# Wave angles as 32-bit integers: one wrapping GpSimd product per tile in place of a two-step turn on GpSimd and VectorE

## The chip, the cores and the metric

The kernel runs on one core of one Trainium2 chip. The metric is the device time of one execution in microseconds (us). A core has five engines that run their own instruction streams in order: PE (TensorE, matrix products), DVE (VectorE), ACT (ScalarE), POOL (GpSimd) and SP (SyncE, which here only issues DMAs). They wait for each other through semaphores.

## The reference, cut to what matters

Sixteen images of 3 x 512 x 512 are cut into 1024 patches each, embedded to 256 features, and go through one transformer layer: attention with 8 heads of 32, then a small mixture of networks. What is unusual is the key. Before attention every key element x (1024 tokens x 256 features per image) is replaced by a Fourier sum over 256 frequencies:

```python
h = patches(x) @ W.T + b
q, k, v = split(layernorm(h) @ w_qkv)
k = sum(a[f] * sin((f + 1) * k) + b[f] * cos((f + 1) * k) for f in range(256))
h = h + softmax(q @ k.T / sqrt(32)) @ v @ w_out + b_out      # 8 heads
h = h + shared_mlp(layernorm(h)) + top2_experts(layernorm(h))
```

The kernel writes a frequency as a slow part (16 steps) and a fast part (8 steps), so that 16 x 16 products of slow and fast waves give all 256 terms.

## The kernel before, in words

**Tiles of waves.** The key's angle, as a fraction of a turn, is stored in DRAM (`ud`) as `u` and as `uh = u + 0.5` (lines 256 to 271, here called the key chunks: four per image, each 128 x 512, a chain of eight DVE instructions and two stores from SP's queue). Four features are one *group*; an image has 32 groups. For each group SP loads three tiles `w` of 128 x 1024 (lines 507 to 525): the same eight rows, repeated over the partitions. Two are for slow waves (one DMA each), the third for fast waves (two DMAs of 64 partitions). There are 12 buffers `w`, which is four groups.

**Turning a tile.** Each partition has its own frequency `f`. A tile must become `f*u` less its whole part. That takes two steps: `begin_turns` (L544) computes `t = w*f + ROUND` on POOL (or on DVE for some tiles), which leaves the nearest whole number in the low bits of `t`; `end_turns` (L534) computes `w*f - whole` on DVE. `t` has two buffers, so POOL cannot be more than two tiles ahead of DVE. Then ACT takes the sine (L556), PE mixes the slow waves with the coefficients (`mix`, L562, into one of two PSUM buffers `big`), DVE multiplies by the fast wave (`times_fast`, L572, which also frees that PSUM buffer), and PE adds up (`add_up`, L588).

**Rounds.** The main loop (lines 714 to 782) is an order written out by hand; each engine executes its instructions in this program order. One round is four groups and one attention step (two heads, half of the queries). An image has eight rounds, numbered 0 to 7 below. A round has a *sine phase* (for each group: three sines, `mix`, `times_fast`, `add_up`, and the loads that refill the freed buffers) and an *exponential phase* (eight steps of `score` L610, `exponential` L620, `weigh` L628). The attention step of two rounds earlier is used, so that keys are always a little ahead. In the exponential phase the tiles of the next round are turned: ten by POOL and DVE there, two by DVE alone in the sine phases of groups 1 and 2.

**Beginning of a round.** After the first three sines ACT copies the finished attention sums out of PSUM (`leave`, L642), and POOL copies two stripes of 32 x 512 of it (L644). In every second round (0, 2, 4, 6) DVE then normalizes (`normalize`): a reciprocal (L653), four products of 32 x 512 (L656) and one more pass (L661). These stand ahead of the first `times_fast` of the round on DVE.

**Pieces.** Everything else (the embedding of the next image, its layernorms, the key chunks, the networks of the image before) is cut into pieces that are slipped between these steps: the networks and their gate in rounds 2 to 5, the next image's tokens and key chunks in rounds 5 to 7. A layernorm uses POOL for a power (L189) and for adding a row (L210), and DVE for four scalings `hn` (L193).

Of the kernel before, what the change touches and what calls it, by code (L numbers as in the profile page):

```python
# [11 lines left out]
FP = mybir.dt.float32  # L12
AF = mybir.ActivationFunctionType
ALU = mybir.AluOpType
# [4 lines left out]
P = 128  # L19
E = 256  # L20
NPAIR = 4
HD = 32
N = 1024
# [14 lines left out]
TURN = 6.283185  # L38

ROUND = 1.5 * 2.0**23  # L40
BAND0 = 88
XT = 256
XBUFS = 2
# [2 lines left out]
NW = 12  # L46
GS = 4
# [4 lines left out]
def plain_path(ctx: ExitStack, tc: tile.TileContext, a: dict, out: bass.AP, verdict: bass.AP):  # L52
# [8 lines left out]
    nc = tc.nc  # L61
# [8 lines left out]
    const = pool("const", 1)  # L70
# [3 lines left out]
    udp = pool("udp", 2, DRAM)  # L74
    kup = pool("kup", 1)
    wp = pool("wp", NW)
    tp = pool("tp", 2)
# [11 lines left out]
    def load(shape, src, name):  # L89
        t = const.tile(shape, FP, tag=name, name=name)  # L90
        nc.sync.dma_start(out=t, in_=src)
        return t
# [29 lines left out]
    sel = load([NE, 2, P], a["sel"], "sel")  # L122
    gw = load([P, 2, NE], halves(a["gW"]), "gw")
    gbr = row_everywhere(a["gb"], NE, "gbr")
    lane = load([P, 2], a["waves"], "lane")
    f_slow, f_fast = lane[:, 0:1], lane[:, 1:2]
    pack = load([P, PACK0 + HD], a["pack"], "pack")
    ident = const.tile([P, P], FP, tag="ident", name="ident")
    make_identity(nc, ident)
# [84 lines left out]
    def tokens(b, st):  # L214

        hs = st["h"] = []
        for half in range(2):
            h = hp.tile([P, 4, E], FP, tag="h", name="h")
            hs.append(h)
            for pr in range(2):  # L220
                ps = side_tile("tok").rearrange("p (t e) -> p t e", e=E)
                for t in range(2):
                    j, col = divmod((4 * half + 2 * pr + t) * P, XT)
                    for c in range(NKC):
                        nc.tensor.matmul(  # L225
                            out=ps[:, t, :],
                            lhsT=chunks[b, j][:, c, ds(col, P)],
                            rhs=wt[:, c, :],
                            start=(c == 0),
                            stop=(c == NKC - 1),  # L230
                        )
                    if col + P == XT:
                        del chunks[b, j]
                        load_x(b, j + XBUFS)
                    yield
                nc.vector.tensor_add(
                    h[:, ds(2 * pr, 2), :], ps, tokb.unsqueeze(1).to_broadcast([P, 2, E])
                )
            yield from transposed_layernorm(h, half)
            add_row(h, bout)  # L240


        ud = st["ud"] = udp.tile([E // 4, 2, 4, N], FP, tag="ud", name="ud")
        for rows in range(2):
            for blk in range(2):
                ps = side_tile("k")
                for c in range(2):
                    nc.tensor.matmul(
                        out=ps,
                        lhsT=wk[:, c, ts(rows, P)],  # L250
                        rhs=hnT[:, c, ts(blk, 512)],
                        start=(c == 0),
                        stop=(c == 1),
                    )
                yield
                n = kup.tile([P, 512], FP, tag="n", name="turns")
                nc.vector.tensor_scalar(n, ps, INV_2PI, ROUND, ALU.mult, ALU.add)
                nc.vector.tensor_scalar(n, n, ROUND, None, ALU.subtract)
                r = kup.tile([P, 512], FP, tag="r", name="r")
                nc.vector.scalar_tensor_tensor(r, n, -TWO_PI_A, ps, ALU.mult, ALU.add)  # L260
                nc.vector.scalar_tensor_tensor(r, n, -TWO_PI_B, r, ALU.mult, ALU.add)
                nc.vector.scalar_tensor_tensor(r, n, -TWO_PI_C, r, ALU.mult, ALU.add)
                u = kup.tile([P, 512], FP, tag="u", name="u")
                nc.vector.tensor_scalar(u, r, INV_2PI_REST, None, ALU.mult)
                nc.vector.scalar_tensor_tensor(u, r, INV_2PI, u, ALU.mult, ALU.add)
                uh = kup.tile([P, 512], FP, tag="n", name="uh")
                nc.vector.tensor_scalar(uh, u, 0.5, None, ALU.add)
                for i, x in enumerate((uh, u)):
                    nc.sync.dma_start(
                        out=ud[ts(rows, P // 4), i, :, ts(blk, 512)], in_=x  # L270
                    )
            st["rows"] = rows + 1
        yield
# [228 lines left out]
    total = B * NG  # L502
    w_tiles = {}
    w_turns = {}
    ptr = {"load": 0, "turn": 0, "used": 0}

    def load_waves():

        while ptr["load"] < min(3 * total, ptr["used"] + NW):
            i = ptr["load"]  # L510
            g, j = divmod(i, 3)
            b, g = divmod(g, NG)
            st = images.get(b)
            if st is None or st.get("rows", 0) <= g // (NG // 2):
                return
            w = wp.tile([P, N], FP, tag="w", name="w")
            for s in range(1 + j // 2):
                m = 16 // (1 + j // 2)
                src = st["ud"][2 * g + (s if j == 2 else j)].rearrange("f e n -> (f e) n")
                nc.sync.dma_start(  # L520
                    out=w[ds(8 * m * s, 8 * m), :],
                    in_=src.unsqueeze(0).to_broadcast([m, 8, N]),
                )
            w_tiles[i] = w
            ptr["load"] += 1

    late = []

    def end_turns():

        while late:
            w, t, f = late.pop(0)
            whole = t.bitcast(mybir.dt.int16)[:, ::2]
            nc.vector.scalar_tensor_tensor(w, w, f, whole, ALU.mult, ALU.subtract)  # L534

    def begin_turns(engine):
        i = ptr["turn"]
        if i >= 3 * total:
            return
        assert i in w_tiles, i  # L540
        w = w_tiles[i]
        f = f_fast if i % 3 == 2 else f_slow
        t = tp.tile([P, N], FP, tag="t", name="t")
        engine.tensor_scalar(t, w, f, ROUND, ALU.mult, ALU.add)  # L544
        late.append((w, t, f))
        ptr["turn"] += 1


    kan = {}
    red = {}  # L550

    def sines(g):
        assert ptr["turn"] >= 3 * g + 3 and not late
        for j in range(3):
            w = w_tiles[3 * g + j]
            nc.scalar.activation(w, w, AF.Sin, scale=TURN)  # L556

    def mix(g):
        ps = kan[g] = big.tile([P, N], FP, tag="big", name="kan")
# [76 lines left out]
    def leave(qb):  # L636

        av = acc[0]
        if qb == 0:
            acc["sums"] = ffp.tile([P, 512], FP, tag="sums", name="sums")  # L640
        acc["v", qb] = ff2.tile([P, 512], FP, tag="avs", name="avs")
        nc.scalar.copy(acc["v", qb], av)  # L642
        for s in range(2):
            nc.gpsimd.tensor_copy(  # L644
                acc["sums"][ds(64 * qb + HD * s, HD), :],
                acc["v", qb][ds(HD + HD * s, HD), :],
            )
# [27 lines left out]
        load_x(0, j)  # L675
    run(tokens(0, image(0)))
    load_waves()
    for i in range(10):
        begin_turns(nc.vector)
        end_turns()  # L680

    RI = NG // GS
    plan = {"gen": None, "left": 0, "slots": 0, "need": None}
# [30 lines left out]
    with tc.manual_schedule():  # L714
        for rd in range(rounds + 2):
# [20 lines left out]
            for n, g in enumerate(groups):  # L736
                sines(g)
                if n == 0 and att > 0:
                    leave(qq)
                mix(g)  # L740
                if n == 0 and att > 0 and qq == 1:
                    normalize(pp)
                if n > 0:
                    times_fast(groups[n - 1])
                    add_up(groups[n - 1])
                    load_waves()
                if n in (1, 2):
                    end_turns()
                    begin_turns(nc.vector)
                    end_turns()  # L750
                piece("sin")
            if not groups and att > 0:
                leave(qq)
# [6 lines left out]
            for n in range(NT):  # L760
                if 0 <= att < 2 * NPAIR * B:
                    score(p, qb, n)
                    exponential(n)
                if n == 0 and groups:
                    add_up(g)
                if n == 2 and groups and g % 8 == 7:
                    finish_keys(g // 8)
                if 0 <= att < 2 * NPAIR * B and n >= 2:
                    weigh(p, qb, n - 2)
                end_turns()  # L770
                for _ in range(2 if n in (3, 7) else 1):
                    if ptr["turn"] < 3 * min(total, GS * (rd + 2)):
                        end_turns()
                        begin_turns(nc.gpsimd)
                piece("exp")
            if 0 <= att < 2 * NPAIR * B:
                for n in (6, 7):
                    weigh(p, qb, n)
            end_turns()
        leave(1)  # L780
        normalize(NPAIR * B - 1)
        run(networks(B - 1, images[B - 1]))
# [667 lines left out]
def _waves():  # L1450

    lane = np.arange(128)
    return np.stack([16.0 * (lane // 8) + 8.5, lane % 64 // 8 + 0.5], 1).astype(np.float32)


def _pack():
# [60 lines left out]
```

## Time and profile before

| what | value |
|---|---|
| times of three runs | 6951.01, 6960.5, 6960.35 us; median 6960.35 us |
| the profiled execution | 6941.8 us, of which the span from first to last instruction is 6940.3 us |
| busy: PE, DVE, ACT, POOL | 87%, 62%, 48%, 33% of the span |
| granted TensorE clock, mean | 0.913 |
| DMA queue of SP | 54.7% of 16 engines' span, 842.66 MB |
| turning, POOL part (L544) | 1270 instructions, 1820.9 us |
| turning, DVE part (L534 and L544) | 1536 and 266 instructions, 2229.2 and 219.6 us |
| copies of the attention sums on POOL (L644) | 256 instructions, 185.5 us |

How to read it: a busy share says how long an engine had an instruction in work, not that it set the time; PE's ends are modelled. The mean duration of a group mixes instructions that ran freely with some that were held up by another engine. A wait is put down to the engine whose result came last.

### The profile page before, as it was taken

To read this page: it belongs to the slowest core of one execution; us is meant where nothing else is said; L and a number is where in the kernel's file an instruction comes from. 1 tells how busy PE (TensorE), PEld (TensorE's weight loads), DVE (VectorE), ACT (ScalarE), POOL (GpSimd) and SP (SyncE) were. 2 spreads that over 40 slices of the span, in tenths; PEclk is the share of its full clock that TensorE was granted. 3 is DMA by queue.
4 is the path that set the end of the run, shared out by engine and by line. 5 is a ranking of instruction groups with operands and counts; after the bars stand their busy time and mean duration, and the time that the engine had idled before them with its cause. 6 is when DMAs were issued, how large, how long until landed. Compare 5 with 4: busy or idle time off the path is not lost.

```text
span 6940.3 us, 62611 instructions
## 1 busy us (share of the span) xinstructions
PE 6014.1 (87%) x21377; PEld 2081.1 (30%) x21377; DVE 4301.0 (62%) x4785; ACT 3319.5 (48%) x3773; POOL 2274.3 (33%) x1728
## 2 busy tenths in 40 slices
PE   5788888888898989989889898898988889888898
PEld 2223323233232323323233232332323323233223
DVE  4675665756657566565765657666575665756652
ACT  2364454544545445454453544545454454544553
POOL 2343333323323333332333323334232332333330
PEclk7899999999999989999899998999989899998998
DMA  6575564655656565565655755556566564655650
GB/s 163 143 166 131 128 148 114 153 114 140 148 114 151 111 144 135 130 151 111 146 126 128 155 115 139 130 124 149 124 143 131 123 147 112 155 124 122 147 123 10
DMA packets 264922, 913.86 MB, mean 132 GB/s; under 512 B 31241, under 2 KB 35218, under 8 KB 264594
## 3 DMA queue, kind: packets, MB, share of 16 engines
q1 hardware_dynamic: 246674, 842.66, 54.7%
q0 software_dynamic: 17920, 67.12, 3.3%
q8 instruction: 171, 2.80, 0.2%
q14 instruction: 157, 1.29, 0.1%
HBM read 859.32 MB, written 50.33 MB: 131 GB/s over the span
## 4 chain that ended last, share of the span: by engine, by line
PE 52%; DVE 15%; DMA 12%; issue 7%; ACT 7%; POOL 6%; SPq 0%; POOLq 0%; ACTq 0%; DVEq 0%
DMA w<-ud 11%; PE sT L610 10%; PE kan L562 8%; PE av L628 7%; PE red L588 6%; PE tok L225 5%; PE e3p L486 4%; PE e1p L411 3%; DVE rc L653 3%; POOL t L544 3%; ACT w L556 3%; DVE aT L656 2%; PE s1p L411 2%; PE q L279 2%; DVE w L534 1%
## 5 line engine op out<-in xcount | busy, mean ns | idle before, releaser
L544 POOL TENSOR_SCALAR t<-w,lane 128x1024 f32<-128x1024 f32 x1270 | 1820.9, 1439 | 2718.5 <-DVE w L534 1866.5
L534 DVE SCALAR_TENSOR_TENSOR w<-w,lane,t 128x1024 f32<-128x1024 f32 x1536 | 2229.2, 1471 | 719.8 <-POOL t L544 710.7
L620 ACT ACTIVATE es<-sT 128x1024 f32<-128x1024 f32 x1024 | 1041.9, 1023 | 2025.4 <-PE sT L610 2023.5
L556 ACT ACTIVATE w<-w 128x1024 f32<-128x1024 f32 x1536 | 1512.3, 1048 | 499.7 <-DVE w L534 495.0
L562 PE MATMUL kan<-w,coef 128*64 128x512 f32 x4096 | 1205.0, 643 | 111.0 <-ACT w L556 110.9
L610 PE MATMUL sT<-q,k 32*128 32x512 f32 x4096 | 1214.7, 671 | 21.8 <-ACT es L620 21.8
L628 PE MATMUL av<-es,v 128*64 128x512 f32 x4096 | 1129.9, 647 | 0.0
L588 PE MATMUL red<-prod,pack 128*32 128x512 f32 x2048 | 610.1, 678 | 502.0 <-DVE prod L572 501.4
L572 DVE TENSOR_TENSOR prod<-kan,w 128x1024 f32<-128x1024 f32 x512 | 625.4, 1221 | 513.4 <-PE kan L562 510.6
L562 PEld LDWEIGHTS kan<-w,coef 128*64 128x64 f32 x4096 | 305.4, 144 | 924.8 <-issue 497.9
L610 PEld LDWEIGHTS sT<-q,k 32*128 32x128 f32 x4096 | 320.0, 191 | 702.7 <-issue 518.7
L628 PEld LDWEIGHTS av<-es,v 128*64 128x64 f32 x4096 | 229.4, 141 | 778.0 <-issue 762.6
L653 DVE RECIPROCAL rc<-sums 128x512 f32<-128x512 f32 x64 | 214.6, 3353 | 389.3 <-POOL sums L644 389.3
L644 POOL COPY sums<-avs 32x512 f32<-32x512 f32 x256 | 185.5, 725 | 731.6 <-ACT avs L642 724.0
L620 ACT ACT_TABLE_LOAD x126 | 161.7, 1283 | 518.0 <-PE sT L610 517.4
L225 PE MATMUL tok<-wt,x 128*128 128x256 f32 x1536 | 394.5, 410 | 13.0 <-DMA x<-in_xT 12.5
L588 PEld LDWEIGHTS red<-prod,pack 128*32 128x32 f32 x2048 | 77.3, 113 | 944.0 <-DVE prod L572 625.5
L225 PEld LDWEIGHTS tok<-wt,x 128*128 128x128 f32 x1536 | 304.3, 205 | 169.1 <-issue 85.1
L411 PE MATMUL e1p<-hnT,w1e 128*128 128x512 f32 x512 | 271.5, 656 | 14.0 <-ACT e L471 12.9
L544 DVE TENSOR_SCALAR t<-w,lane 128x1024 f32<-128x1024 f32 x266 | 219.6, 826 | 10.5 <-DMA w<-ud 10.4
L496 POOL DMA_DIRECT2D out<-h x32 | 26.5, 828 | 591.1 <-DVE h L495 564.2
L495 DVE TENSOR_TENSOR h<-e3p,h 128x512 f32<-128x512 f32 x64 | 44.3, 692 | 269.5 <-PE e3p L486 269.5
(98 smaller groups left out, 4327.7 us busy)
## 6 DMA issues: line engine op xcount, KB each, us to landing
w<-ud SPq DMA_DIRECT2D x1024, 512.0 KB
w<-ud SPq DMA_DIRECT2D x1024, 256.0 KB
x<-in_xT POOLq DMA_DIRECT2D x64, 768.0 KB, 8.3
ud<-u SPq DMA_DIRECT2D x64, 256.0 KB
ud<-uh SPq DMA_DIRECT2D x64, 256.0 KB
out<-h POOLq DMA_DIRECT2D x32, 512.0 KB, 7.5
wt<-in_tok_wT SPq DMA_DIRECT2D x1, 768.0 KB
w1e<-in_eW SPq DMA_DIRECT2D x1, 512.0 KB
```

The costliest lines, as they stand in the source:

```text
L225: nc.tensor.matmul(out=ps[:, t, :], lhsT=chunks[b, j][:, c, ds(col, P)], rhs=wt[:, c, :], start=(c == 0), stop=(c == NKC - 1),)
L411: nc.tensor.matmul(out=ps, lhsT=lhsT(c), rhs=hnT[:, c, cols], start=(c == 0), stop=(c == 1),)
L534: nc.vector.scalar_tensor_tensor(w, w, f, whole, ALU.mult, ALU.subtract)
L544: engine.tensor_scalar(t, w, f, ROUND, ALU.mult, ALU.add)
L556: nc.scalar.activation(w, w, AF.Sin, scale=TURN)
L562: nc.tensor.matmul(out=ps[ts(j, 64), ts(blk, 512)], lhsT=coef, rhs=w_tiles[3 * g + j][:, ts(blk, 512)], start=True, stop=True,)
L572: nc.vector.tensor_mul(prod, kan.pop(g), w_tiles[3 * g + 2])
L588: nc.tensor.matmul(out=rows_of_pair[p][ds(64 * blk + HD * (r // 4), HD), :], lhsT=pack[:, o : o + HD], rhs=prod[:, ts(blk, 512)], start=(r ...
L610: nc.tensor.matmul(out=ps[:, ts(s, 512)], lhsT=k[rows, ts(kc, P)], rhs=q[p % NPAIR // 2][rows, ts(qb, 512)], start=True, stop=True,)
L620: nc.scalar.activation(es, scores.pop(kc), AF.Exp, scale=SCALE)
L628: nc.tensor.matmul(out=acc[0][ts(s, 64), :], lhsT=v[:, kc, p % NPAIR, ds(HD * s, 64)], rhs=es[:, ts(s, 512)], start=(kc == 0), stop=(kc == ...
L653: nc.vector.reciprocal(rc, sums)
```

## The change

- The angle is kept as a 32-bit integer, a full turn being 2^32. In each key chunk the last DVE instruction makes `ui = u * 2^31` with an integer output (half a turn per unit), and `uh = ui + 2^30` is now an integer addition on POOL.
- A tile is turned by one instruction on POOL: the integer product `w * f`, where `f` is one odd integer per partition, broadcast along the tile. It is meant to wrap at 32 bits, which drops the whole turns. `begin_turns`, `end_turns`, the tiles `t` and all turning on DVE are gone.
- ACT reads the integer tile and scales by 2*pi/2^32.
- The order changes: all 12 tiles of the first round are turned ahead of the loop; then one tile is turned in each sine phase of groups 2 and 3, and ten in the exponential phase (steps 6 and 7 turn two). All of these are POOL's.
- The two copies of the attention sums in `leave` move from POOL to DVE.

```diff
-                uh = kup.tile([P, 512], FP, tag="n", name="uh")
-                nc.vector.tensor_scalar(uh, u, 0.5, None, ALU.add)
-                for i, x in enumerate((uh, u)):
+                ui = kup.tile([P, 512], INT, tag="r", name="ui")
+                nc.vector.tensor_scalar(ui, u, 2.0**31, None, ALU.mult)
+                uh = kup.tile([P, 512], INT, tag="n", name="uh")
+                nc.gpsimd.tensor_tensor(uh, ui, quarter.to_broadcast([P, 512]), ALU.add)
+                for i, x in enumerate((uh, ui)):
...
-    def end_turns():
-        while late:
-            w, t, f = late.pop(0)
-            whole = t.bitcast(mybir.dt.int16)[:, ::2]
-            nc.vector.scalar_tensor_tensor(w, w, f, whole, ALU.mult, ALU.subtract)
-    def begin_turns(engine):
...
-        t = tp.tile([P, N], FP, tag="t", name="t")
-        engine.tensor_scalar(t, w, f, ROUND, ALU.mult, ALU.add)
-        late.append((w, t, f))
+    def turn_waves(n):
+        for _ in range(n):
...
+            f = lane[:, i % 3 // 2 : i % 3 // 2 + 1]
+            nc.gpsimd.tensor_tensor(w, w, f.to_broadcast([P, N]), ALU.mult)
...
-            nc.scalar.activation(w, w, AF.Sin, scale=TURN)
+            x = w_tiles[3 * g + j] = w.bitcast(FP)
+            nc.scalar.activation(x, w, AF.Sin, scale=TURN * 2.0**-32)
...
-            nc.gpsimd.tensor_copy(
+            nc.vector.tensor_copy(
                 acc["sums"][ds(64 * qb + HD * s, HD), :],
...
-    for i in range(10):
-        begin_turns(nc.vector)
-        end_turns()
+    turn_waves(NW)
...
-                if n in (1, 2):
-                    end_turns()
-                    begin_turns(nc.vector)
-                    end_turns()
+                if n >= 2:
+                    turn_waves(1)
...
-                end_turns()
-                for _ in range(2 if n in (3, 7) else 1):
-                    if ptr["turn"] < 3 * min(total, GS * (rd + 2)):
-                        end_turns()
-                        begin_turns(nc.gpsimd)
+                if ptr["turn"] < 3 * min(total, GS * (rd + 2)):
+                    turn_waves(2 if n > 5 else 1)
```

## The prediction

> **What bounds the kernel now.** The busy shares come first (the page's first part), then PE's own waits, then the eight rounds of one image as windows, then the rows of the instructions that the change touches.
>
> ```profile
> PE 6014.1 (87%) x21377; PEld 2081.1 (30%) x21377; DVE 4301.0 (62%) x4785; ACT 3319.5 (48%) x3773; POOL 2274.3 (33%) x1728
> ```
> ```profile
> PE red L588 <- DVE prod L572: 501.4, 96, 15.3
> PE kan L562 <- ACT w L556: 110.9, 128, 10.4
> PE wT L429 <- DVE gwt L354: 104.4, 16, 6.6
> PE lnT L205 <- DVE hn L193: 83.0, 65, 7.3
> PE k L248 <- DVE r L260: 56.2, 15, 5.7
> ```
> PE is the bound: only 6940 - 6014 = 926 us are idle. Over half of that is one wait, `red` for `prod`, 96 times: six per image. The 111 us on ACT are 128 waits of 0.9 us, one per round, at the change from exponentials to sines; they stay.
>
> Windows of one image, rounds 0, 1, 4 and 7 (busy PE, PEld, DVE, ACT, POOL; then granted clock, DMA share, GB/s):
> ```profile
> 3010.50:3056.20 45.70, 36.16 (x124) 9.61 (x124) 32.59 (x27) 23.76 (x25) 19.83 (x14) 0.93 0.75 161
> 3056.20:3092.60 36.40, 35.48 (x144) 11.14 (x140) 19.32 (x16) 25.62 (x34) 12.35 (x11) 1.00 0.74 157
> ...
> 3204.90:3270.30 65.40, 58.94 (x193) 19.35 (x190) 33.91 (x30) 29.16 (x35) 16.05 (x13) 0.95 0.50 105
> ...
> 3394.90:3437.50 42.60, 32.91 (x120) 7.93 (x116) 30.57 (x31) 24.36 (x27) 15.62 (x11) 0.88 0.68 151
> ```
> Round 1 has no PE idle to give; rounds 0 and 7 have about 10 us each. The image takes 427.0 us with PE busy 375.4.
>
> The rounds that normalize all look like round 4 (timeline):
> ```profile
> 3207.74 0.56 ACT L642 COPY avs<-av 128x512 f32<-128x512 f32 x1
> 3208.44 1.25 POOL L644 COPY sums<-avs 32x512 f32<-32x512 f32 x2 [14.66 <-ACT avs L642]
> 3209.72 3.35 DVE L653 RECIPROCAL rc<-sums 128x512 f32<-128x512 f32 x1 [14.62 <-POOL sums L644]
> 3213.11 2.80 DVE L656 TENSOR_TENSOR aT<-avs,rc 32x512 f32<-32x512 f32 x4
> ...
> 3217.16 1.22 DVE L572 TENSOR_TENSOR prod<-kan,w 128x1024 f32<-128x1024 f32 x1
> ...
> 3218.43 1.92 PE L588 MATMUL red<-prod,pack 128*32 128x512 f32 x4 [5.63 <-DVE prod L572]
> ```
> Both PSUM buffers hold unread mixes, so PE stands 5.63 us until DVE has normalized and made the first `prod`. No turn stands in this chain; the turns follow it, under a busy PE.
>
> **What goes from DVE and what comes to POOL.** Gone from DVE: 2229 + 220 = 2449 us. Most of it was under PE's cover, so this sum is not the gain. To POOL come 1536 products of 128x1024. No row shows one. The nearest row is POOL's own two-operand addition of that size (L210); the one-operand step (L544) ran freely at 1.12:
> ```profile
> L210 POOL TENSOR_TENSOR h<-h,bout x32: 2337/2348/2357, 33.1 to 6363.7; 128x1024 f32<-128x1024 f32 x32
> L656 DVE TENSOR_TENSOR aT<-avs,rc x256: 678/683/690, 318.7 to 6841.5; 32x512 f32<-32x512 f32 x128
> ```
> I take 2.35 us. The ends are 1.12 (as one operand) and 4.70 (an estimate: two passes of the addition). At 2.35 POOL carries 2274 - 1821 - 186 + 3610 + 75 (64 half-size additions for `uh`, 1.17 each) = 3950 us, 57% of the span: not a bound. Within a round, twelve products are 28.2 us, while SP's loads bring twelve tiles in some 37 us (round 1's run from 3060 to 3097); POOL waits for tiles and not the reverse.
>
> **The place where it costs.** So far POOL's step ran only when DVE let it, because of the two buffers `t`. During normalization DVE was busy and POOL stood: none of 256 `aT` products, 678 to 690 ns, met a POOL instruction. Now nothing ties the products to DVE. What a meeting costs the trace shows at other places:
> ```profile
> 3373.61 2.35 POOL L210 TENSOR_TENSOR h<-h,bout 128x1024 f32<-128x1024 f32 x1
> 3373.68 3.37 DVE L534 SCALAR_TENSOR_TENSOR w<-w,lane,t 128x1024 f32<-128x1024 f32 x1 [1.02 <-POOL t L544]
> ...
> 3175.52 1.12 POOL L544 TENSOR_SCALAR t<-w,lane 128x1024 f32<-128x1024 f32 x1 [14.58 <-DVE rank L378]
> 3175.62 1.05 DVE L379 TENSOR_TENSOR gwt<-gwt,rank 128x32 f32<-128x32 f32 x1
> ```
> The DVE instruction (1.28 alone) ended 1.1 us after the POOL addition did; a 0.19 us operation took 1.05. A DVE instruction with two SBUF operands stands until the POOL instruction beside it is done, then they alternate. So it went with `hn` also, which has one SBUF operand (1.23 for 0.40 beside L544 at 3362.9). `prod`, with one operand in PSUM, was never lengthened (1210 to 1226).
>
> Round 4, step by step. The first two tiles of the next round are loaded when the first mix has read their buffers (issue 3208.4 and 3209.1) and land at 3212.1 and 3214.4 by the trace's DMA packets. The copies on DVE: 3208.3 + 2 x 0.43 (L267, one operand) = 3209.2; reciprocal to 3212.6, 0.5 us earlier than now. First product 3212.2 to 3214.6; first `aT` to 3215.1; second product to 3217.5; second `aT` to 3218.0; two more `aT`, L661 and one product of the networks 2.8 us; `prod` starts at 3220.8 instead of 3217.2. **Plus 3.6 us**, all PE idle. The third tile waits for `prod`, so two meetings are the limit. In round 6 the tiles land at 3342.7 and 3345.1: by the same steps **plus 4.0**. In round 2 late tiles of round 1 come on top and meet the copies, which are taken to be held as `hn` was: 4.0 to 6.3, **plus 5.0**. In round 0 the old POOL copies waited too (3.4 us in the instance at 3440), which is gained, but up to four products meet the chain: 0 to 6, **plus 4.4**. Sum 17.0 us per image.
>
> The Trainium skill (SBUF — State Buffer, Who interferes with whom) says that a DVE copy can enter a two-port mode and then stands against GpSimd as well. No DVE copy is in this trace. By that rule the copies in rounds 0 to 2 wait as taken here; without it the sum would be some 3 us per image lower, 7210 us.
>
> **Other terms, per image.** Layernorms: of four `hn` two were held up to 1.23 instead of 0.40; beside a 2.35 us product it is 1 us more on PE's wait for `lnT`, four times: **plus 4**. Gate (round 3): DVE leaves out one L534 (1.3) and the hold of L379 (0.85), but meets one product (2.35): **0**. Round 1, which has no slack: two DVE copies ahead of `prod` while late tiles are turned: 0 to 3, **plus 1**. Round 7: three L534 stood between the last key chunk (ends 3404.7) and the first `prod` (3409.8); 5.1 us go. In return `uh` comes from POOL, 1.2 us later in each of three chunks, since the next chunk waits for its store: 3.6. **Minus 1.5**. `ui` with an integer output: 0.43 to 0.69, at most 1 us. Behind the last `uh` SP's next loads are queued; they start about as now. If L556 reads integers at its 1.05 us, nothing; twice that would fill ACT's idle half and bind the sine phase. The prologue (12 products against 10 turns on DVE, both behind loads): 0 to 5 us once.
>
> The sum is 17 + 4 + 0 + 1 - 1.5 = plus 20.5 us per image. The first image lacks two attention steps: 15.5 x 20.5 = 318. On the profiled execution's 6941.8 that is **7260 us**; the median of the runs lies 19 us above the profile, less than the sum's uncertainty.
>
> The clock: the gaps of 3.5 to 8.8 us are each followed by half clock for 7 to 10 us. If longer gaps each bring the 10, that is 1.7 us more of PE time, four times: up to 105 us in all, on the high side. The Trainium skill (TensorE: Matmul & The Clock Gate, What's actually happening) has the array at half rate after one idle window of some 3.4 us and back after one busy window; by it the present gaps already pay, and this term is zero.
>
> **Rivals.** *No meetings (faster).* If an integer product with a broadcast factor doesn't hold DVE up, or the tiles land after the `aT`, what is left are the savings: round 0 2.7, rounds 2, 4, 6 0.5 each, gate 2.1, round 7 1.5 to 5.1: 7.8 to 11.4 per image, 6765 to 6820 us; some clock with it, down to 6720. It decides when the two products cost the chain under 1 us. For it: 501 us of waiting are there to be taken. Against: L210 held L534 for its whole length.
>
> *POOL's rate (much slower).* POOL needs 12 products and 2.7 us of other work per round. That equals my mean round of 56 us at 4.4 us a product; short rounds suffer from 3.6 us. At 5 us: 62.7 x 8 = 502 per image, 8100 us. Against: an addition takes 2.35. For: nothing shows what a 32-bit multiplication costs.
>
> *The product doesn't wrap.* Then the change doesn't do what it says, and the time is the same, since no step depends on the values. The Trainium skill (GPSIMD Engine Reference, Engine selection) names only the integer addition as exact.
>
> **How the numbers follow.** Meetings 0.46 (7050 to 7500), POOL's rate 0.20 (above 7500), no meetings 0.28 (6600 to 6930), savings and meetings cancelling 0.06. Within 0.2% (14 us, about what a measurement here can tell from no change) 0.04; faster 0.28; slower 0.68. The range 6720 to 7800 leaves out the fastest tenth and products above 4.6 us.
>
> **What would show it.** The product's row at 2.35; `aT` with a maximum near 3 us and a mean over 1.2; PE's wait of `red` for `prod` grown from 501 towards 750; DVE's wait for POOL's `sums` gone; round 4 near 69 us. Wrong if `aT` stays at 683 (then 6790), or if ACT's sines wait for POOL's products (then POOL's rate).

## The result: 5% slower, with the products standing in the way of VectorE's instructions

The changed kernel takes 7319.82 us (median of 4, 7291.92 to 7324.02), the kernel before 6955.68 us beside it: ratio 1.052, interval 1.0487 to 1.0553. The profiled execution took 7319.39 us with a span of 7317.8.

The page of the changed kernel, its first part and its row of the products, and PE's waits:

```profile
PE 6098.8 (83%) x21377; PEld 2108.5 (29%) x21377; DVE 2512.3 (34%) x3239; ACT 3310.1 (45%) x3773; POOL 3212.8 (44%) x1803
...
L540 POOL TENSOR_TENSOR w<-w,lane 128x1024 int32<-128x1024 int32 x1536 | 2924.7, 1917 | 2219.5 <-DMA w<-ud 1812.4
```
```profile
PE red L584 <- DVE prod L568: 630.8, 93, 21.0
PE lnT L208 <- DVE hn L196: 248.3, 150, 6.6
PE wT L434 <- DVE gwt L359: 140.8, 16, 15.5
PE kan L558 <- ACT w L552: 115.8, 133, 11.1
```

VectorE lost 1789 us of work (4301 to 2512) and the kernel became longer. Nothing is near saturation but PE, and PE stands more: its idle time rose from 926 to 1219 us. The product itself is cheaper than was thought (1.88 us when it runs freely), and POOL, at 44%, stands longest for tiles that have not landed (1812 us on `w<-ud`, of 4105 us idle). PE's three largest waits are all for VectorE, which is now idle two thirds of the time: VectorE is not short of time, it is held up.

Round 4 after the change (timeline), the chain that was shown of before:

```profile
3374.52 0.56 ACT L638 COPY avs<-av 128x512 f32<-128x512 f32 x1
3375.12 0.85 DVE L640 COPY sums<-avs 32x512 f32<-32x512 f32 x2 [32.28 <-ACT avs L638]
3376.00 3.35 DVE L649 RECIPROCAL rc<-sums 128x512 f32<-128x512 f32 x1
3379.39 6.08 DVE L652 TENSOR_TENSOR aT<-avs,rc 32x512 f32<-32x512 f32 x4
3380.02 4.19 POOL L540 TENSOR_TENSOR w<-w,lane 128x1024 int32<-128x1024 int32 x2 [23.47 <-ACT w L552]
...
3386.72 2.34 DVE L568 TENSOR_TENSOR prod<-kan,w 128x1024 f32<-128x1024 f32 x2
...
3387.99 1.92 PE L584 MATMUL red<-prod,pack 128*32 128x512 f32 x4 [8.41 <-DVE prod L568]
```

The copies are quicker, as forecast. The four `aT` took 2.80 us before and take 6.08 now, because exactly two products (4.19 us) run between them. PE's gap is 8.41 us where it was 5.63.

The same at a layernorm of round 2:

```profile
3296.67 1.02 POOL L192 TENSOR_TENSOR rstd<-ve,mhalf 128x4 f32<-128x4 f32 x1 [17.82 <-PE sT L606]
3297.66 11.34 POOL L540 TENSOR_TENSOR w<-w,lane 128x1024 int32<-128x1024 int32 x6
3297.72 7.67 DVE L196 TENSOR_SCALAR hn<-h,mv,rstd 128x256 f32<-128x256 f32 x4 [1.13 <-POOL rstd L192]
...
3301.66 0.33 PE L208 MATMUL lnT<-ident,hn 128*128 128x128 f32 x1 [1.57 <-DVE hn L196]
```

POOL stood 17.82 us at the layernorm's power, whose input was not ready (the bracket names PE, but `ve`, its input, was written by VectorE only at 3296.6). Meanwhile six tiles landed. When the power was done, the six products ran back to back, at the very moment at which VectorE wanted its four `hn`; each `hn` got through between two products. In the layernorms of rounds 5 and 6 the power itself waits only 2.1 and 0.2 us (at 3486 and 3536), and six and four products follow all the same. There POOL had stood just before at another instruction of its queue, the issue of the next input load `x` (L176), which waits for PE: 5.1 and 14.7 us. In the kernel before POOL stood at the same places, but with two buffers `t` only two turns could follow, and two of four `hn` were held. The image's remaining layernorm, whose `hn` start 9 to 10 us after the power, meets no product after the change (0.41 us each).

The instructions by source line (minimum/median/maximum ns):

```profile
L652 DVE TENSOR_TENSOR aT<-avs,rc x256: 678/687/2407, 308.6 to 7216.9; 32x512 f32<-32x512 f32 x128
L196 DVE TENSOR_SCALAR hn<-h,mv,rstd x256: 404/1977/1990, 31.3 to 7234.5; 128x256 f32<-128x256 f32 x128
L640 DVE COPY sums<-avs x256: 414/419/2056, 228.5 to 7210.9; 32x512 f32<-32x512 f32 x128
L568 DVE TENSOR_TENSOR prod<-kan,w x512: 1206/1224/1226, 88.3 to 7158.4; 128x1024 f32<-128x1024 f32 x171
```

`hn` needs 0.40 us and in the median takes 1.98, a whole product and a little more; 180 of 256 are held. `prod`, one of whose operands lies in PSUM, was never held up in 512 times, though 170 of them began while a product was running. The Trainium skill (SBUF — State Buffer, Who interferes with whom) says just this of the three kinds: two SBUF operands stand against GpSimd, a one-operand copy or scaling in its two-port mode also, one operand from SBUF without that mode does not. The rows agree, the copy's maximum of 2056 ns included; the mode itself is not to be seen in the trace.

**The rounds.** Mean length in us of each round from the first sine to the next round's, over the third to the fifteenth image of each profiled execution, worked out from the traces; the kernels are described below. A row belongs to one execution, which for the hold at normalization was the fastest of four (39 us below the median).

| kernel | 0 | 1 | 2 | 3 | 4 | 5 | 6 | 7 | sum |
|---|---|---|---|---|---|---|---|---|---|
| before | 45.3 | 36.4 | 55.1 | 57.8 | 64.7 | 62.4 | 61.9 | 43.0 | 426.6 |
| after | 46.0 | 36.4 | 64.3 | 60.8 | 67.0 | 66.2 | 66.1 | 45.1 | 451.9 |
| no product | 42.7 | 36.4 | 51.2 | 56.2 | 64.0 | 56.6 | 58.0 | 42.8 | 407.9 |
| hold at normalization | 46.2 | 36.4 | 61.0 | 57.9 | 63.8 | 66.1 | 63.0 | 45.2 | 439.6 |
| hn on ScalarE | 46.8 | 36.4 | 59.0 | 65.4 | 67.0 | 62.6 | 61.3 | 44.9 | 443.4 |
| product in two halves | 46.1 | 36.4 | 58.5 | 58.9 | 66.8 | 62.7 | 61.8 | 45.2 | 436.4 |
| product twice | 52.2 | 46.7 | 69.0 | 74.3 | 70.0 | 66.3 | 74.6 | 46.1 | 499.2 |
| both holds, uh on VectorE | 46.5 | 36.4 | 53.8 | 62.9 | 65.2 | 60.3 | 66.8 | 31.4 | 423.3 |

### The profile page after: what moved, and what is told of

It is laid out like the page before. It is cut to its first block, busy times and chain, and to the rows that moved or that the text cites. A ratio compares the mean times of both kernels' runs of the same rounds, so it can differ in the third digit from the quotient of the medians.

```text
span 7317.8 us, 60795 instructions
## 1 busy us (share of the span) xinstructions
PE 6098.8 (83%) x21377; PEld 2108.5 (29%) x21377; DVE 2512.3 (34%) x3239; ACT 3310.1 (45%) x3773; POOL 3212.8 (44%) x1803
## 5 line engine op out<-in xcount | busy, mean ns | idle before, releaser
L540 POOL TENSOR_TENSOR w<-w,lane 128x1024 int32<-128x1024 int32 x1536 | 2924.7, 1917 | 2219.5 <-DMA w<-ud 1812.4
L552 ACT ACTIVATE w<-w 128x1024 f32<-128x1024 int32 x1536 | 1503.3, 1048 | 307.4 <-POOL w L540 301.1
L606 PE MATMUL sT<-q,k 32*128 32x512 f32 x4096 | 1241.3, 684 | 22.0 <-ACT es L616 22.0
L624 PE MATMUL av<-es,v 128*64 128x512 f32 x4096 | 1155.4, 660 | 0.0
L640 DVE COPY sums<-avs 32x512 f32<-32x512 f32 x256 | 147.1, 574 | 2126.4 <-ACT avs L638 2124.2
L196 DVE TENSOR_SCALAR hn<-h,mv,rstd 128x256 f32<-128x256 f32 x256 | 371.8, 1512 | 40.7 <-POOL rstd L192 40.1
L208 PE MATMUL lnT<-ident,hn 128*128 128x128 f32 x512 | 149.3, 386 | 248.9 <-DVE hn L196 248.3
L652 DVE TENSOR_TENSOR aT<-avs,rc 32x512 f32<-32x512 f32 x256 | 339.3, 1325 | 6.9
L176 POOL DMA_DIRECT2D x<-in_xT x64 | 54.9, 858 | 569.8 <-PE tok L228 569.8
L272 POOL TENSOR_TENSOR uh<-ui,quarter 128x512 int32<-128x512 int32 x64 | 69.0, 1078 | 451.0 <-DVE ui L270 439.8
```

What stands on the lines that cost most here:

```text
L196: nc.vector.tensor_scalar(hn[:, t, :], h[:, t, :], mv[:, t, 0:1], rstd[:, t : t + 1], ALU.subtract, ALU.mult,)
L540: nc.gpsimd.tensor_tensor(w, w, f.to_broadcast([P, N]), ALU.mult)
L552: nc.scalar.activation(x, w, AF.Sin, scale=TURN * 2.0**-32)
L606: nc.tensor.matmul(out=ps[:, ts(s, 512)], lhsT=k[rows, ts(kc, P)], rhs=q[p % NPAIR // 2][rows, ts(qb, 512)], start=True, stop=True,)
L624: nc.tensor.matmul(out=acc[0][ts(s, 64), :], lhsT=v[:, kc, p % NPAIR, ds(HD * s, 64)], rhs=es[:, ts(s, 512)], start=(kc == 0), stop=(kc == ...
L652: nc.vector.tensor_mul(aT[ds(64 * (i % 2) + HD * s, HD), i // 2, ts(qb, 512)], acc["v", qb][ds(num, HD), :], rc[ds(64 * qb + HD * s, HD), :],)
```

## The experiments

The theory, by that rule, is that a product on POOL holds a port which VectorE needs for every instruction with two SBUF operands and for its fast one-operand form, and that PE waits for those. The rivals are POOL's rate, and the other edits (copies, `uh`, order). All ratios are to the kernel before on the same chip.

**1. Without the products**

```diff
-            nc.gpsimd.tensor_tensor(w, w, f.to_broadcast([P, N]), ALU.mult)
```


> The changed kernel with the 1536 products on GpSimd left out (the tiles go unturned to the sine, so the keys are not the reference's). Theory (the products stand on the port that VectorE's two-operand and fast one-operand instructions need): everything that was lengthened is short again: aT at 683 ns, hn at 0.40 us, and the time falls below the kernel before, by the savings that remain (copies on VectorE, no turn on VectorE): 6941.8 less 8 to 11 us per image, 6770 to 6820 us. Rival (the other edits cost it: copies on VectorE, uh on GpSimd, the new order): the time stays above 7000 us.

Measured 6649.1 us, ratio 0.9559 (0.9539 to 0.958). Source lines and PE's first wait:

```profile
L651 DVE TENSOR_TENSOR aT<-avs,rc x256: 678/683/690, 289.1 to 6541.7; 32x512 f32<-32x512 f32 x128
L196 DVE TENSOR_SCALAR hn<-h,mv,rstd x256: 403/407/416, 31.4 to 6560.9; 128x256 f32<-128x256 f32 x128
```
```profile
PE red L583 <- DVE prod L567: 410.9, 97, 12.9
```

All other edits are still in, and the kernel is 302 us below the one before: the other edits are not what costs, the products cost 671 us. This run also leaves POOL's rate out, so it doesn't tell the theory from that rival. That it is far below the 6770 expected is a miss: the two-step turns had cost more than the waits charged to them (see the rivals below).

**2. Products held back until the normalization is done**

```diff
+        hold = smp.tile([P, 1], FP, tag="hold", name="hold")
+        nc.gpsimd.tensor_copy(hold, sums[:, 0:1])      # behind the last pass of normalize
```


> The changed kernel with one small copy (128x1) on GpSimd that reads the output of the normalization's last pass; it holds back the products of the next round's first tiles until VectorE has normalized. Theory: the aT products no longer meet them (maximum 0.69 us but for late tiles in rounds 0 and 2), the gap of TensorE in rounds 2, 4 and 6 goes from 7.5, 8.4 and 4.9 us to some 5, 5 and 3.5: 7 us less per image and 110 us in all, about 7210 us. Rival (GpSimd's rate sets the time): holding GpSimd back makes it slower than 7320 us.

Measured 7163.98 us, ratio 1.0306 (1.028 to 1.0332): 156 us less than the changed kernel, by making POOL wait. The wait:

```profile
PE red L584 <- DVE prod L568: 505.8, 94, 17.8
```

That is the 501 of before. Rounds 2, 4 and 6 become 3.1 to 3.3 us shorter; round 3 also, by 2.9, but that is the gate, which varies by itself (see below). Round 0 does not move, where what meets the chain are late tiles of round 7, which stand ahead of the hold. Had POOL's rate set the time, this would have cost.

**3. hn on ScalarE**

```diff
-            nc.vector.tensor_scalar(hn[:, t, :], h[:, t, :], mv[:, t, 0:1], rstd[:, t : t + 1], ALU.subtract, ALU.mult)
+        nc.vector.scalar_tensor_tensor(shift, mv[:, :, 0], -1.0, rstd, ALU.mult, ALU.mult)
+            nc.scalar.activation(hn[:, t, :], h[:, t, :], AF.Identity, bias=shift[:, t : t + 1], scale=rstd[:, t : t + 1])
```


> The changed kernel with the layernorm's scaling hn moved from VectorE to ScalarE, which has its own way to the memory (and a small 128x4 pass on VectorE for its bias). Theory: TensorE's waits of lnT for hn (248 us, three or four gaps of 1.57 us for each half image) fall to below the 83 us of the kernel before: 165 to 200 us less, about 7140 us. Rival (the layernorm is late for another reason, the power on GpSimd behind the products): the wait of lnT stays over 200 us and the time within 50 us of 7320.

Measured 7169.63 us, ratio 1.0306 (1.0284 to 1.0329). PE's wait for `hn` falls from 248 to 90 us; rounds 2, 5 and 6 become 5.3, 3.6 and 4.8 us shorter. The power on GpSimd stands as it did, so it was the hold of `hn` and not a late power. Round 3 becomes 4.6 us longer: ScalarE's extra work delays its sines (PE's wait for them went from 116 to 174 us, and all of the increase is in round 3).

**4. The copies alone, on the kernel before**

```diff
-            nc.gpsimd.tensor_copy(
+            nc.vector.tensor_copy(
```


> The kernel before with one part of the change alone: the two copies of the attention sums on VectorE and not on GpSimd. Theory: VectorE's wait for them (389 us) goes, but the chain of normalization gains only 0.5 us in rounds 2, 4 and 6 and 2 to 3 us in round 0: 4 us per image, 60 us in all, about 6890 us. Rival (the copies meet GpSimd's turns and delay the first prod in the other rounds): 6950 to 7000 us.

Measured 6924.52 us, ratio 0.9956 (0.9942 to 0.997): a gain, but 27 us where 60 were expected. PE's wait of `red` fell from 501 to 468 only.

**5. uh on VectorE again**

```diff
-                nc.gpsimd.tensor_tensor(uh, ui, quarter.to_broadcast([P, 512]), ALU.add)
+                nc.vector.tensor_scalar(uh, u, 2.0**31, 2.0**30, ALU.mult, ALU.add)
```


> The changed kernel with one part undone: the quarter-turn copy uh comes from VectorE again (u times 2^31 plus 2^30, integer output) and not from GpSimd. Theory: each key chunk's store leaves 1.1 us sooner, and the next chunk, which waits for that store, starts sooner; three chunks stand in a row ahead of the first prod of round 7, whose gap goes from 10.8 to some 8 us: 3 to 4 us per image, 50 to 60 us in all, 7260 to 7270 us. Rival (the chunks are late because VectorE is held up by products, not by uh): within 15 us of 7320.

Measured 7297.35 us, ratio 1.0499 (1.0459 to 1.0538), whose interval overlaps that of the changed kernel: not told apart. In the trace round 7 falls by 3.5 us (45.1 to 41.6) as expected, and rounds 3 and 6 grow by 2.6 together. The step is real in its place and worth little in the whole.

**6. Every product twice**

```diff
             nc.gpsimd.tensor_tensor(w, w, f.to_broadcast([P, N]), ALU.mult)
+            nc.gpsimd.tensor_tensor(w, w, unit.to_broadcast([P, N]), ALU.mult)      # unit is 1
```


> The changed kernel with a second product (by 1) on every tile: GpSimd's work per tile doubles to 3.8 us, each single instruction holds the port as long as before. Theory (meetings): in rounds 0, 2, 4 and 6 four products instead of two stand between the aT, 3 to 4 us more each, and rounds 7, 0 and 1 come to be set by GpSimd's rate (12 x 3.8 + 2.7 = 48 us against 45, 46 and 36): 23 to 30 us per image, 7680 to 7800 us. Rival (GpSimd's rate sets the time throughout): every round becomes proportional to it; GpSimd's busy time grows by 2925 us and the time by more than 1000 us, over 8300 us.

Measured 8089.35 us, ratio 1.1648 (1.1628 to 1.1667), between the two forecasts. Round 1, which has no normalization, is 46.7 us: 24 instructions of 1.94. There POOL's rate does bind, as the prediction had it for products over 3.6 us. But rounds 4, 5 and 7 grow by only 3.0, 0.1 and 1.0 us, while POOL's busy time nearly doubles (3213 to 6179 us): the time is not proportional to its work. More meetings are to be seen: of the 16 `aT` of an image 11.5 are held instead of 7.1, and of the 18 gate instructions of VectorE in round 3 nine or ten instead of 2.5. But the sines also wait longer for products (301 to 772 us), and no run separates here how much of the rest is meetings and how much late products. PE's waits:

```profile
PE red L587 <- DVE prod L571: 943.7, 123, 27.0
PE wT L436 <- DVE gwt L361: 305.0, 16, 21.5
PE lnT L210 <- DVE hn L198: 277.9, 164, 7.2
```

**7. Each product cut into two halves**

```diff
-            nc.gpsimd.tensor_tensor(w, w, f.to_broadcast([P, N]), ALU.mult)
+            for c in range(2):
+                wc = w[:, ts(c, 512)]
+                nc.gpsimd.tensor_tensor(wc, wc, f.to_broadcast([P, 512]), ALU.mult)
```


> The changed kernel with each product cut into two of 128x512: the same elements, but VectorE, when it meets one, stands for some 1.0 us and not 1.9. Theory (length of a meeting): hn's median falls from 1.98 to about 1.15 us, the wait of lnT from 248 to some 130 us, the wait of red for prod from 631 to some 560 us, and the time by 150 to 250 us, to 7070 to 7170 us, although GpSimd's busy time grows by 8% (uh at that size takes 1.04 us against half of 1.89). Rival (GpSimd's work or rate): the time grows with it, 7320 to 7400 us.

Measured 7092.55 us, ratio 1.0218 (1.0201 to 1.0235): 227 us less, with more work on POOL. The product's row on the page, a source line and PE's wait for it:

```profile
L542 POOL TENSOR_TENSOR w<-w,lane 128x512 int32<-128x512 int32 x3072 | 3197.2, 1069 | 1905.1 <-DMA w<-ud 1535.6
```
```profile
L196 DVE TENSOR_SCALAR hn<-h,mv,rstd x256: 401/1124/1135, 31.3 to 6996.1; 128x256 f32<-128x256 f32 x128
```
```profile
PE lnT L208 <- DVE hn L196: 108.6, 121, 6.3
```

This is the run that separates the theory from POOL's rate. POOL works 272 us more (3197 against 2925), and the kernel is faster, because what VectorE waits for is the end of *one* instruction: `hn` went from 1977 to 1124 ns, which is the step from a 1.89 us product to a 1.04 us one. The wait of `red` fell less than expected (598, not 560): there are more meetings, 9.9 held `aT` per image instead of 7.1.

**8. Three mends together: hold at the normalization, hn on ScalarE, uh on VectorE**

The edits are those of 2, 3 and 5, unchanged.

> Three mends together: the hold of GpSimd's products until the normalization is done, hn on ScalarE, uh on VectorE. Theory: the three act on different rounds (2, 4, 6; the layernorms; round 7) and add up: 7320 less 156, 150 and 55: about 6960 us, level with the kernel before. Rival (the wait only moves to the next VectorE instruction that meets the held-back products): the sum is not reached, over 7050 us.

Measured 7042.44 us, ratio 1.0147 (1.0129 to 1.0164). The three alone sum to 156 + 150 + 22 = 328 us, which would be 6992; 50 us of that are not reached. `red` is at 427 us, but round 3 stays at 65.0 us with ScalarE's extra load.

**9. Hold at the layernorm**

```diff
         nc.gpsimd.tensor_tensor(rstd, ve, mhalf, ALU.pow)
-        yield
         hn = hnp.tile([P, 4, E], FP, tag="hn", name="hn")
...
+        hold = smp.tile([P, 1], FP, tag="hold", name="hold")
+        nc.gpsimd.tensor_copy(hold, hn[:, 3, 0:1])      # behind the four hn
```


> The changed kernel with the layernorm's four hn issued directly behind the power, and one small copy (128x1) on GpSimd behind them, which holds back the products that have collected behind the power until hn is done. The hn stay on VectorE. Theory: no product stands between the hn (0.40 us each), the wait of lnT for hn falls from 248 to under 90 us, rounds 2, 5 and 6 shorten as with hn on ScalarE, and round 3 is not lengthened as it was there (65.4 us): 150 to 190 us less, 7130 to 7170 us. Rival (GpSimd falls behind by the hold): the sines wait longer for products than the 301 us of the changed kernel, and the time stays over 7250.

Measured 7078.8 us, ratio 1.0168 (1.0143 to 1.0193), 241 us less than the changed kernel; the source line of `hn` and PE's wait:

```profile
L195 DVE TENSOR_SCALAR hn<-h,mv,rstd x256: 405/407/416, 31.3 to 7027.1; 128x256 f32<-128x256 f32 x128
```
```profile
PE lnT L209 <- DVE hn L195: 63.6, 50, 6.1
```

No `hn` of 256 is held up. This gives 185 us of waiting back; the rest of the 241 was not expected. The left-out `yield` makes one piece fewer at each half image, so that the key chunks move from round 7 into round 6 (which now take 33.0 and 71.2 us, 45.1 and 66.1 before it). That is a second change in the same kernel, and no run has the one without the other.

**10 and 11. Both holds and uh on VectorE, then with the products in halves too**

Kernel 10 has the edits of 2, 5 and 9, kernel 11 that of 7 besides.

> Both holds (normalization and layernorm) and uh on VectorE. Theory: as with the three mends before (7042 us), but without ScalarE's extra load in rounds 3 and 6: 7000 us, 6970 to 7030. Rival (what the holds release meets the gate or the next prod's neighbours): over 7050 us.

> Both holds, uh on VectorE, and each product cut into two of 128x512. Theory: what still meets (late tiles in rounds 0 and 2, the gate, the aT's neighbours) costs half: another 60 to 100 us less than without the cut, 6900 to 6950 us, at or below the kernel before. Rival (with the meetings gone the cut only adds GpSimd work): level with the kernel without the cut.

Measured 6886.08 us, ratio 0.9911 (0.9892 to 0.9931), and with halves 6893.05 us, ratio 0.9922 (0.9899 to 0.9945). Both are below both given kernels. Not all of it is the holds: of the 28.6 us per image by which kernel 10 is below the changed kernel, 13.7 lie in round 7, where `uh` (3.5 us in experiment 5) and the earlier key chunks act. With the meetings at the normalizations of rounds 2, 4 and 6 and at the layernorms gone or nearly so, halving the products brings nothing more: the intervals overlap, as the rival said. What is left of `red`:

```profile
PE red L585 <- DVE prod L569: 438.1, 64, 10.6
PE k L252 <- DVE r L264: 146.7, 16, 11.3
PE wT L435 <- DVE gwt L360: 101.9, 16, 8.7
```

**12. Control: the order of 9 in the kernel before, with the copies on VectorE**

```diff
-        yield
...
-            nc.gpsimd.tensor_copy(
+            nc.vector.tensor_copy(
```


> A control for the kernels with the layernorm's hold: the kernel before (two-step turns) with the copies on VectorE and hn issued directly behind the power, which makes one piece fewer for each half image, so that the key chunks end earlier; no integer product. Theory (part of the gain of the held kernels is this order): round 7 shortens from 43 to some 33 us and round 6 grows by less, 3 to 5 us less per image than the 6924 us with the copies alone: 6845 to 6880 us, level with or below the best held kernel (6886). Rival (the order is worth nothing by itself; the holds made the gain): 6910 to 6940 us.

Measured 7074.49 us, ratio 1.0181 (1.0167 to 1.0195): both forecasts fail, it is 150 us slower than with the copies alone. PE's wait for the key chunks (`k` for `r`) is 185 us, where the kernel with the copies alone has 70. So with the two-step turns the order costs. It has this price in kernel 10 too, where the same wait is 147 us against 15 in the changed kernel; what it gives in return there, in the short round 7, was not separated from the holds.

## Why the prediction was right, and by which steps

7260 us was forecast and 7319.82 measured. The mechanism named as decisive, meetings of VectorE's instructions with products, is the one the runs show. That the sum came so close (20.5 us per image, measured as 25.3) is partly luck: its largest term was twice too large, and three smaller ones were too small. The profiled execution became 378 us longer. PE's wait of `red` for `prod` rose by 129 us, its wait for `hn` by 165, its wait for the gate by 36 and its own busy time by 85, while its wait for the key chunks fell by 41. The forecast had 264 us (17.0 per image) for the normalizations, which are the larger part of `red`, and 62 (4 per image) for `hn`.

- **The product's price.** 2.35 us was taken from the addition; it is 1.88 to 1.89 when free. POOL's busy time came out at 3213 us, not 3950. The condition "POOL waits for tiles" held: it stands 1812 us for them.
- **Normalization.** The step is right and its size was not. In the four rounds that normalize, PE's gap before `red` grew by 8.0 us per image where 17.0 were forecast: 0.7, 3.4, 2.6 and 1.3 in rounds 0, 2, 4 and 6 (forecast 4.4, 5.0, 3.6, 4.0). Round 4 has its two meetings (1.85 held `aT` in the mean); some 0.9 us of what is missing is the product's cheaper price (2 x 0.46). Round 6 has one meeting, not two: the `aT` begin at 3514.5, the first tile has landed only at 3516.3, and its product alone reaches them. That round 6 as a whole grew by 4.2 us, near the forecast, is a coincidence: 4.5 us of it are a layernorm. In round 0 the `aT` are lengthened by 2.7 us; without products the gap there is 2.1 us shorter than before (experiment 1), which gains most of it back. Experiment 2 takes the term away in rounds 2, 4 and 6. Round 1 was plus 1 against 0.
- **Round 2** grew by 9.2, not by 5.0 and a layernorm's share of 1: PE's wait for `hn` grew by 3.6 beside the 3.4 above, and PE's own busy time by 2.3.
- **Layernorms** were the undersized term: plus 4 us per image, and PE's wait for `hn` rose by (248 - 83)/16 = 10.3. The step "two of four `hn` are held" is what failed: in three of an image's four layernorms all four are held. It was read from the kernel before, where two buffers `t` let only two turns follow. Now, while POOL stands at the power (round 2) or at the issue of `x` (rounds 5 and 6), every tile that lands collects behind it. Experiments 3, 7 and 9 agree.
- **Gate.** 0 forecast, with one meeting; round 3 plus 3.0, PE's wait for the gate 104 to 141 us. The trace shows why it varies between 55.2 and 68.8 us from image to image: by the number of gate instructions of VectorE that a product holds up. With none held PE waits 4.7 to 5.3 us, with three 9.1 to 9.9, with six 15.5; in the kernel before it is one each time, and 6.6. No run takes these meetings away by themselves.
- **Round 7.** Minus 1.5 forecast, plus 2.1 measured. The charge for `uh`, 3.6, was right: the key chunks begin 8.7 to 9.0 us apart instead of 7.5 to 7.6, and undoing `uh` gave 3.5 us of the round back (experiment 5). The credit was not: with `uh` on VectorE the round is 41.6 us, 1.4 below the kernel before, where 5.1 were credited for the three turns that left.
- **The clock.** Taken as zero, by the reading of the Trainium skill (TensorE: Matmul & The Clock Gate, What's actually happening) that gaps of 3.5 us pay already; the forecast's own reading, half clock for 7 to 10 us after each gap and more after longer ones, allowed 105 us. The granted clock fell from 0.913 to 0.886 and PE's busy time rose by 85 us for the same 21377 matmuls, so the zero was wrong. But it was not the longer gaps at the normalization that cost it. In the trace of before the half-clock stretches at those gaps last 3.4 to 10.2 us, of which 4.5 to 5.5 in the mean lie behind the gap. Where the gap grew from 5.6 to 8.2 us (round 4) and from 9.3 to 10.9 (round 7), PE's busy time did not grow; so far the rows agree with the page. It grew in rounds 2, 3 and 6, by 2.3, 1.4 and 1.3 us per image, where `hn` and the gate wait; with `hn` on ScalarE it is back at its old value in rounds 2 and 6 (49.4 and 54.2 us), though the gap before `red` in round 2 stays at 7.3.
- **Rivals.** POOL's rate: refuted by experiments 2 and 7, except for short rounds with products over 3.6 us (experiment 6). No meetings: its saving of 120 to 175 us was undersized, since kernel 1 is 302 us below. In it `lnT` waits 26 us instead of 83, the clock is 0.935, and rounds 2, 5 and 6 are 3.9 to 5.8 us shorter: POOL's step of the old turns had met the layernorms as well (two of four `hn` at 1.2 us), and without it round 5, for one, runs at a clock of 1.00 instead of 0.91. The product that doesn't wrap: no time here can tell it, and no run was made for it.
- **What was to show it**: `aT`'s maximum 2.4 us and mean 1.33, the wait for POOL's sums gone, round 4 at 67.0 us (69 forecast), `red` at 631 us (750 forecast).

## What to carry to other kernels

An engine's busy share doesn't tell what moving work to it costs; ask which VectorE instructions with two SBUF operands (or in the fast one-operand form) stand in the chains that the bounding engine waits for, and whether GpSimd can now run beside them. A two-engine hand-over that looks like waste can be what kept the two apart: here a two-buffer dependence did. If the work must go to GpSimd, one small instruction that makes it wait until the chain is through gave back 156 us here, and shorter instructions 227. A GpSimd instruction that waits, even one that only issues a load, collects the work behind it and releases it all at once.

## What was not expected of the hardware

- GpSimd's 32-bit integer product of 128x1024 with a per-partition broadcast factor takes 1.88 us, less than its fp32 addition of the same size (2.34 to 2.35 us); an integer addition of 128x512 takes 1.04 us. No run tells the integer type from the broadcast factor.
- ScalarE's sine reads integers at the same price (1046 ns in the median), and VectorE's scaling with an integer output takes 426 ns for 128x512, as the one with an fp32 output did (L267 before).
- The power on 128x4 took 1977 ns in the median before and 1024 after. The hold works both ways: all 45 long ones before began beside a two-operand L534 of VectorE, and the 19 short ones (1.0 us) beside a `prod` or beside nothing.
